# Layer 3 attention of a four-layer network: exponentials turned by block transposes on VectorE and transfers, not by TensorE

## The chip, the cores and the metric

The kernel runs on one core of a Trainium2 chip, which has eight. The metric is the device time of one execution in microseconds (us), as the median of several runs. The profile is of one further execution. The engines of the core are TensorE (PE; its weight loads are shown apart, as PEld), VectorE (DVE), ScalarE (ACT) and GpSimd (POOL). SyncE (SP) computes nothing: it issues transfers (DMAs). Each engine takes its instructions in order from a queue of its own, and they wait for each other by semaphores.

## The reference

The network has four layers on an input of 2 x 512 x 32 x 32 in float32. Layers 0 to 2 are a deformable attention with an MLP, a deformable convolution and a linear attention. The change is in layer 3, an ordinary attention with 8 heads of 64 channels over the 1024 positions of each of the two batch entries:

```python
def _L3_conv_ref(x, gn_scale, gn_bias, W_qkv, b_qkv, W_out, b_out, num_heads):
    ...
    h = _group_norm(x, gn_scale, gn_bias)
    h = jnp.einsum('bchw,cd->bdhw', h, W_qkv) + b_qkv[None, :, None, None]
    h = h.reshape(B, num_heads, 3 * hd, H * W).transpose(0, 1, 3, 2)
    q, k, v = jnp.split(h, 3, axis=-1)
    scale = 1.0 / jnp.sqrt(jnp.asarray(hd, dtype=q.dtype))
    logits = jnp.einsum('bhsd,bhtd->bhst', q, k) * scale
    attn = jax.nn.softmax(logits, axis=-1)
    vals = jnp.einsum('bhst,bhtd->bhsd', attn, v)
    h = vals.transpose(0, 1, 3, 2).reshape(B, C, H, W)
    h = jnp.einsum('bchw,cd->bdhw', h, W_out) + b_out[None, :, None, None]
    return x + h
```

The softmax runs over the keys, so logits are made with queries on the partitions and keys along the row. The product with the values sums over keys, and TensorE sums over partitions. Between the two, each 128 x 1024 block of exponentials has to be turned: keys on the partitions, queries along the row.

## The kernel before, in words

Layers run one after another, with loads and small pieces of the next layer woven in. Layer 3 is the method `heads` of the class `Attention`, called by `layer3`. Its work is a list of 64 items `(b, hp, s0)`: a batch entry, a pair of heads (`hp`, 0 to 3) and 128 queries from `s0`. First come the 32 items of batch entry 0, then those of entry 1. Two items in a row share 256 queries of one pair of heads.

The order of TensorE's instructions is that of the program. That of the other engines is made by a planner of the framework, which goes by what it reckons to be ready, and among what is ready by the order in the program. `issue_after` tells it to queue something behind a given instruction.

One turn of the loop, for item `at`, does this:

- `logits` (L1988) of item `at + 1`: four products of 128 queries with 512 keys, two for each of the two heads, into two tiles `pl` of 128 x 1024 in PSUM. The pool `ps_l` has two such tiles, so the next logits wait until the exponentials of both heads have been read from them.
- `maximum` (L2078) on VectorE: the row maximum of each `pl`, negated.
- `exponentials` (L2086) on ScalarE: exp(pl - max) into a tile `e` in SBUF, with the row sum in `s`.
- `divide` on VectorE: the reciprocal of `s` (L2090) and the row times it (L2091).
- Four groups `g` of four transposes on TensorE (L2040) of item `at`, two groups for each head. Each group goes through a tile `pt` of PSUM and is copied to `aT` in SBUF, by VectorE for one group (L2049) and by ScalarE for three (L2051).
- Behind each group a share of `fill`: other work of TensorE that the stage needs anyway, namely the second batch entry's normalization (L1816 to L1885), values (L1898), queries and keys (L1921), and the output projection (L1951). Its results go through `spare`, one bank of PSUM, and are moved out by VectorE and ScalarE. The projection's results are stored by SP (L1964).
- `weigh` (L2003) once for two items: eight tiles of keys, two heads, with `aT` as the moving operand of 256 queries. The first half runs behind the logits of one turn, the second half behind those of the next. A copy on ScalarE (L2013) takes the result away.

SP has almost nothing to do in this stage: one load of weights and 20 stores.

Of the kernel before, what the change touches and what calls it, by code (L numbers as in the profile page):

```python
# [10 lines left out]
F32 = mybir.dt.float32  # L11
AF = mybir.ActivationFunctionType
ALU = mybir.AluOpType
# [6 lines left out]
HW = 1024  # L20
# [256 lines left out]
def layers(net, out):  # L277
# [12 lines left out]
    with ExitStack() as later:  # L290
# [101 lines left out]
        with ExitStack() as l1:  # L392
# [92 lines left out]
            with ExitStack() as ctx:  # L485
# [5 lines left out]
                for i, _ in enumerate(linear.run(1, bank, held)):  # L491
                    some(keys, 2)
                    some(values, BESIDE[i])
                some(keys, 99)
        layer3(net, att, later, values, banks, out)


# [1339 lines left out]
class Attention:  # L1837
# [129 lines left out]
    def open_heads(self, ctx):  # L1967
        net = self.net
        self.tmp = net.pool(ctx, "l3_tmp", 2)
        self.ps_l = net.psum(ctx, "l3_logits", 2)  # L1970
        self.ps_t = net.psum(ctx, "l3_turn", 2)
        self.ps_o = net.psum(ctx, "l3_out", 1)

    def heads(self, work, first, fill):

        net, nc = self.net, self.net.nc  # L1980
        ident = net.cst("ident")

        def logits(b, hp, s0):
            q, key = self.qk[b, hp, 0], self.qk[b, hp, 1]
            pls = [self.ps_l.tile([128, HW], F32, name="pl", tag="pl") for _ in range(2)]
            for n in range(2):
                for r, pl in zip((0, 64), pls):
                    nc.tensor.matmul(  # L1988
                        pl[:, half(n)],
                        lhsT=q[r : r + 64, s0 : s0 + 128],  # L1990
                        rhs=key[r : r + 64, half(n)],
                        start=True,
                        stop=True,
                    )
            return [(pl, self.maximum(pl)) for pl in pls]

        def weigh(b, hp, s0, aTs):

            po = self.ps_o.tile([128, 256], F32, name="po3", tag="po3")
            for t in range(8):  # L2000
                for r, aT in zip((0, 64), aTs):
                    c0 = 128 * hp + r
                    nc.tensor.matmul(  # L2003
                        po[r : r + 64, :],
                        lhsT=self.v[b][:, t, c0 : c0 + 64],
                        rhs=aT[:, t, :],
                        start=(t == 0),
                        stop=(t == 7),
                        skip_group_check=True,
                    )  # L2010
                if t == 3:
                    yield
            nc.scalar.copy(self.qk[b, hp, 0][:, s0 : s0 + 256], po)  # L2013
            yield

        done = 0
        fill = list(fill)
        weighing = iter(())
        ahead = [self.exponentials(*part) for part in logits(*work[0])]
        for e in ahead:  # L2020
            self.divide(*e)
        for _ in first:
            pass
        for at, (b, hp, s0) in enumerate(work):
            now, ahead = [e for e, _ in ahead], []
            if at + 1 < len(work):
                one, other_one = logits(*work[at + 1])
                ahead.append(self.exponentials(*one))
            next(weighing, None)
            if at % 2 == 0:  # L2030
                aTs = [
                    self.tmp.tile([128, 8, 256], F32, name="aT", tag="aT", bufs=4)
                    for _ in range(2)
                ]
            for g in range(4):
                e, aT = now[g // 2], aTs[g // 2]
                pt = self.ps_t.tile([128, 512], F32, name="pt3", tag="pt3")
                for c in range(4):
                    k = 4 * (g % 2) + c
                    nc.tensor.transpose(  # L2040
                        pt[:, 128 * c : 128 * c + 128], e[:, 128 * k : 128 * k + 128], ident
                    )
                c0 = 128 * (at % 2)
                dst = aT[:, 4 * (g % 2) : 4 * (g % 2) + 4, c0 : c0 + 128]
                src = pt.rearrange("p (c s) -> p c s", s=128)


                if g == 1:
                    evicted = nc.vector.tensor_copy(dst, src)  # L2049
                else:  # L2050
                    evicted = nc.scalar.copy(dst, src)  # L2051
                if ahead and g < 2:
                    with net.tc.issue_after(evicted.ins):
                        if g == 0:
                            ahead.append(self.exponentials(*other_one))
                        else:
                            self.divide(*ahead[1])
                    if g == 0:
                        self.divide(*ahead[0])
                if fill:  # L2060
                    steps, other, count = fill[0]
                    done += 1
                    for _ in range(done * count // (4 * steps) - (done - 1) * count // (4 * steps)):
                        next(other, None)
                    if done == 4 * steps:
                        for _ in other:
                            pass
                        fill.pop(0)
                        done = 0
            if at % 2 == 1:  # L2070
                weighing = weigh(b, hp, s0 - 128, aTs)
        for _ in weighing:
            pass

# [3 lines left out]
        self.net.nc.vector.tensor_reduce(m, pl, AX.X, ALU.max, negate=True)  # L2078
        return m

    def exponentials(self, pl, m):

        nc = self.net.nc
        e = self.tmp.tile([128, HW], F32, name="e3", tag="e3", bufs=4)
        s = self.tmp.tile([128, 1], F32, name="s3", tag="s3", bufs=4)
        nc.scalar.activation(e, pl, AF.Exp, bias=m, accum_out=s)  # L2086
        return e, s

    def divide(self, e, s):
        self.net.nc.vector.reciprocal(s, s)  # L2090
        self.net.nc.vector.tensor_scalar(e, e, s, None, ALU.mult)  # L2091

    def last_bank(self, name):
        return self.ps_t.tile([128, 512], F32, name=name, tag="pt3")
# [2 lines left out]
def layer3(net, att, ctx, values, banks, out):  # L2097


    att.open_heads(ctx)  # L2100
    ps_f = net.psum(ctx, "l3_fill", 1)

    def spare(name):
        return ps_f.tile([128, 512], F32, name=name, tag="fill")

    first = [(0, hp, s0) for hp in range(CC) for s0 in range(0, HW, 128)]
    second = [
        (1, hp, begin + s0)
        for begin, size in ((0, 512), (512, 256), (768, 256))
        for hp in range(CC)  # L2110
        for s0 in range(0, size, 128)
    ]
# [51 lines left out]
```

## Time and profile before

| | us |
|---|---|
| median of 3 runs | 3835.34 (3830.59 to 3837.44) |
| span of the profiled execution | 3835.8 |
| first logits of layer 3 to the end of the span | 3290 to 3836 |
| in these 546 us: PE busy | 528.5 |
| DVE busy | 332.0 |
| ACT busy | 274.3 |
| POOL busy | 0 |

All of the change lies in the last 546 us. The costs of its instructions are read from groups of the same line and shape, and the pace of the stage from the spacing of the logits, which start once for each item. A busy engine in the table is one that has an instruction running; a matmul's end is modelled.

### The profile page before, as it was taken

Reading aid. Unit: us, or ns where it says so; the run is one execution under the profiler, and the core shown is the slowest. Engines: PE = TensorE matmul, PEld = TensorE weight load, DVE = VectorE, ACT = ScalarE, POOL = GpSimd, SP = SyncE. Lnnn points to the kernel's source line nnn. Section 1 sums busy time; section 2 is a strip of 40 time slices with the busy share of each in tenths; the row PEclk is TensorE's granted clock in tenths of the full one; section 3 lists DMA queues with packets and bytes.
Section 4 is the critical chain, followed back from the end, with each engine's and each line's share of the span. In section 5 each row is a group of like instructions: output and inputs, shape, how many; then the busy total and the mean of one; then the engine's idle time right before and its main releaser. Section 6 shows DMA issues by size and latency. Waiting matters only on the chain. (4 is left out here: it accounts for less than half of the span.)

```text
span 3835.8 us, 59384 instructions
## 1 busy us (share of the span) xinstructions
PE 3739.0 (97%) x25356; PEld 1487.3 (39%) x25356; DVE 2765.5 (72%) x3242; ACT 2566.4 (67%) x2941; POOL 189.1 (5%) x180
## 2 busy tenths in 40 slices
PE   7999999999999999999999999999979999899999
PEld 4532222223222322232323444444434544455555
DVE  6999999999999999999999210411475472566565
ACT  7999999999999999999999221211123243345544
POOL 0000000000000000000000000000261150000000
PEclk9999999999999999999999999999999999999999
DMA  3000000000000000000000100112455481000000
GB/s 111 1 23 23 23 1 23 23 23 12 12 23 23 12 12 23 23 12 12 23 23 34 61 0 0 40 61 77 143 185 173 140 276 42 1 12 1 1 20 25
DMA packets 54459, 168.57 MB, mean 44 GB/s; under 512 B 4804, under 2 KB 10436, under 8 KB 51252
## 3 DMA queue, kind: packets, MB, share of 16 engines
q1 hardware_dynamic: 31556, 83.77, 6.2%
q0 software_dynamic: 21776, 79.14, 6.2%
q8 instruction: 200, 3.28, 0.4%
q10 hardware_dynamic: 864, 1.86, 0.2%
q14 instruction: 63, 0.52, 0.0%
HBM read 156.11 MB, written 8.65 MB: 43 GB/s over the span
## 5 line engine op out<-in xcount | busy, mean ns | idle before, releaser
L888 PE MATMUL ph<-h,w_t 128*32 128x512 f32 x16384 | 1808.0, 593 | 15.7 <-ACT lo L898 6.5
L868 DVE TENSOR_TENSOR h<-ab 128x1024 f32<-128x1024 f32 x1024 | 1206.0, 1219 | 67.2 <-PE ph L888 66.2
L888 PEld LDWEIGHTS ph<-h,w_t 128*32 128x32 f32 x16384 | 547.6, 110 | 1239.9 <-issue 1017.2
L877 ACT ACTIVATE h<-h 128x1024 f32<-128x1024 f32 x832 | 872.1, 1067 | 45.6 <-DVE h L868 42.9
L901 DVE SCALAR_TENSOR_TENSOR hi<-lo,low_w,hi 128x1024 f32<-128x1024 f32 x512 | 654.8, 1279 | 31.6 <-ACT hi L900 30.3
L900 ACT ACTIVATE hi<-ph,size_b,size 128x1024 f32<-128x1024 f32 x512 | 621.3, 1214 | 16.7 <-PE ph L888 12.5
L898 ACT ACTIVATE lo<-ph,vec_t 128x1024 f32<-128x1024 f32 x512 | 571.8, 1117 | 5.8 <-PE ph L888 5.4
L2086 ACT ACTIVATE e<-pl,m 128x1024 f32<-128x1024 f32 x128 | 143.6, 1122 | 228.9 <-DVE m L2078 228.9
L1567 PE MATMUL po<-fold,turned 128*128 128x512 f32 x576 | 266.1, 606 | 3.2 <-DVE dfacc L1575 2.9
L2078 DVE TENSOR_REDUCE m<-pl 128x1 f32<-128x1024 f32 x128 | 150.7, 1219 | 147.2 <-PE pl L1988 147.2
L1135 ACT ACTIVATE h<-ph,vec_t 128x512 f32<-128x512 f32 x64 | 44.0, 687 | 312.0 <-PE ph L1127 311.5
L909 PE MATMUL sim<-hi,w 128*32 128x512 f32 x2048 | 251.0, 592 | 0.0
L1127 PE MATMUL ph<-xn,room 128*128 128x512 f32 x512 | 230.9, 594 | 0.0
L1116 PE MATMUL acc<-h,mlp_w_t 128*128 128x512 f32 x512 | 229.8, 592 | 0.0
L1514 DVE SCALAR_TENSOR_TENSOR sum<-got,wts,sum 128x256 f32<-128x256 f32 x432 | 184.4, 478 | 48.8 <-ACT sum L1510 46.4
L1490 POOL DMA_INDIRECT got<-table,idx x144 | 175.0, 1215 | 554.9 <-DVE sum L1514 268.0
L2040 PE MATMUL pt<-cst_t,e 128*128 128x128 f32 x1024 | 149.3, 279 | 6.6 <-ACT aT L2051 4.0
L2040 PEld LDWEIGHTS pt<-cst_t,e 128*128 128x128 f32 x1024 | 118.6, 142 | 93.6 <-issue 61.3
L1567 PEld LDWEIGHTS po<-fold,turned 128*128 128x128 f32 x576 | 106.6, 195 | 112.4 <-issue 107.4
L1116 PEld LDWEIGHTS acc<-h,mlp_w_t 128*128 128x128 f32 x512 | 97.3, 190 | 122.5 <-issue 122.0
L1127 PEld LDWEIGHTS ph<-xn,room 128*128 128x128 f32 x512 | 96.6, 191 | 117.7 <-issue 117.1
L1541 ACT COPY turned<-pt 128x512 f32<-128x512 f32 x72 | 41.9, 582 | 143.8 <-PE pt L1535 143.6
(250 smaller groups left out, 2711.6 us busy)
## 6 DMA issues: line engine op xcount, KB each, us to landing
ab<-feat_d SPq DMA_DIRECT2D x64, 512.0 KB, 4.0
room<-in_dc_w_dram SPq DMA_DIRECT2D x9, 1024.0 KB, 4.8
dc_w_t<-in_dc_w_dram SPq DMA_DIRECT2D x5, 1024.0 KB, 5.3
room<-in_mlp_w_dram SPq DMA_DIRECT2D x1, 4096.0 KB, 15.6
mlp_w_t<-in_mlp_w_dram SPq DMA_DIRECT2D x1, 4096.0 KB, 12.5
dc_w_t<-in_dc_w_dram SPq DMA_DIRECT2D x8, 512.0 KB, 5.0
w_qkv_t<-in_w_qkv_dram SPq DMA_DIRECT2D x3, 1024.0 KB, 8.6
out_dram<-x_all SPq DMA_DIRECT2D x12, 256.0 KB, 2.0
```

Of the source, the lines that this page charges most:

```text
L868: nc.vector.tensor_tensor(h1.rearrange("p (y x) -> p y x", x=32), at_x[:, k : k + 1, :].to_broadcast([128, 32, 32]), at_y[:, k, :].unsquee ...
L877: nc.scalar.activation(h1, h1, AF.Relu)
L888: nc.tensor.matmul(ph[32 * t : 32 * t + 32, half(n)], lhsT=w2[:, c0 : c0 + 32], rhs=pair[t // 2][:, half(n)], start=True, stop=True, skip_ ...
L898: nc.scalar.activation(lo, phs[0], AF.Relu, bias=b2_lo)
L900: nc.scalar.activation(hi, phs[1], AF.Relu, bias=size_b, scale=size)
L901: nc.vector.scalar_tensor_tensor(hi, lo, low_w, hi, ALU.mult, ALU.add)
L909: nc.tensor.matmul(sim[32 * t : 32 * t + 32, half(n)], lhsT=w3[:, 30 - j : 62 - j], rhs=sums[t][:, half(n)], start=(j == 0), stop=(j == 30 ...
L1116: nc.tensor.matmul(accs[oc], lhsT=self.w2[:, m, 128 * oc : 128 * oc + 128], rhs=hs[m], start=(m == 0), stop=(m == 15),)
L1127: nc.tensor.matmul(ph, lhsT=self.w1[:, k, 128 * m : 128 * m + 128], rhs=xn[:, k, :], start=(k == 0), stop=(k == CC - 1),)
L1514: nc.vector.scalar_tensor_tensor(t[:, q, :], g[:, s, :], w, t[:, q, :], ALU.mult, ALU.add)
L1567: nc.tensor.matmul(self.out, lhsT=turned[:, at : at + 128], rhs=self.folded.w[k][:, i, :], start=(k == 0 and i == 0), stop=(k == 8 and i = ...
L2040: nc.tensor.transpose(pt[:, 128 * c : 128 * c + 128], e[:, 128 * k : 128 * k + 128], ident)
```

## The change

TensorE's transposes and their evictions are left out. For each item a new inner function `attend` now makes logits, maxima, exponentials and the division, and then turns both heads' rows:

- ScalarE writes the exponentials in another order, so that the 32-key blocks which will land on the same 32 partitions lie side by side.
- ScalarE divides, in place of VectorE.
- VectorE transposes every 32 x 32 block of the row in place (`nc.vector.transpose`).
- SP moves the blocks to their partitions: 16 transfers for an item, each from 32 partitions to 32 others, two heads of 256 numbers (1 KB) each, 64 KB in all. They go into a tile `aT` that holds two items and two heads.

Both heads' exponentials lie in one tile `e2`, of which there are two buffers; `aT` has two as well. `weigh` reads `aT` with blocks of 32 queries as its inner run. Its first half runs behind the logits of the first of two turns and its second half two groups later in the same turn. The result's pool `ps_o` has two buffers instead of one, and the fill uses the two banks of `ps_t`, which have become free, instead of one of its own.

```diff
-        self.ps_o = net.psum(ctx, "l3_out", 1)
+        self.ps_o = net.psum(ctx, "l3_out", 2)
...
+        turned = {}
...
-            return [(pl, self.maximum(pl)) for pl in pls]
+            return pls
+
+        def attend(at):
+
+            if at % 2 == 0:
+                turned[at // 2] = self.tmp.tile([128, 2, 2, 4, 256], F32, name="aT", tag="aT")
+            e2 = self.tmp.tile([128, 2, HW], F32, name="e3", tag="e3")
+            for r, pl in enumerate(logits(*work[at])):
+                m = self.maximum(pl)
+                e = e2[:, r, :]
+                self.divide(e, self.exponentials(e, pl, m))
+                nc.vector.transpose(e, e)
+            for a in range(4):
+                for u in range(4):
+                    nc.sync.dma_start(
+                        out=turned[at // 2][32 * u : 32 * u + 32, :, at % 2, a, :],
+                        in_=e2[32 * a : 32 * a + 32, :, 256 * u : 256 * u + 256],
+                    )
...
-                        rhs=aT[:, t, :],
+                        rhs=aT[:, r, :, :, 32 * t : 32 * t + 32].rearrange("p s a q -> p (s a) q"),
...
-        ahead = [self.exponentials(*part) for part in logits(*work[0])]
-        for e in ahead:
-            self.divide(*e)
+        attend(0)
         for _ in first:
             pass
         for at, (b, hp, s0) in enumerate(work):
...
             if at + 1 < len(work):
-                one, other_one = logits(*work[at + 1])
-                ahead.append(self.exponentials(*one))
+                attend(at + 1)
             next(weighing, None)
...
             for g in range(4):
-                e, aT = now[g // 2], aTs[g // 2]
-                pt = self.ps_t.tile([128, 512], F32, name="pt3", tag="pt3")
-                for c in range(4):
...
-                if g == 1:
-                    evicted = nc.vector.tensor_copy(dst, src)
-                else:
-                    evicted = nc.scalar.copy(dst, src)
...
+                if g == 2:
+                    next(weighing, None)
                 if fill:
...
-                weighing = weigh(b, hp, s0 - 128, aTs)
+                weighing = weigh(b, hp, s0 - 128, turned.pop(at // 2))
...
+    def exponentials(self, e, pl, m):
+
+        s = self.tmp.tile([128, 1], F32, name="s3", tag="s3", bufs=4)
+        self.net.nc.scalar.activation(
+            e.rearrange("p (u c k) -> p c u k", u=4, k=32),
+            pl.rearrange("p (c u k) -> p c u k", u=4, k=32),
+            AF.Exp,
+            bias=m,
+            accum_out=s,
+        )
+        return s
+
+    def divide(self, e, s):
         nc = self.net.nc
...
+        nc.vector.reciprocal(s, s)
+        nc.scalar.activation(e, e, AF.Copy, scale=s)
...
-    ps_f = net.psum(ctx, "l3_fill", 1)
-
-    def spare(name):
-        return ps_f.tile([128, 512], F32, name=name, tag="fill")
+    spare = att.last_bank
```

More of the change, by code (lines that the diff above doesn't have):

```diff
@@ L1971, in open_heads @@
         self.ps_t = net.psum(ctx, "l3_turn", 2)
-        self.ps_o = net.psum(ctx, "l3_out", 1)
+        self.ps_o = net.psum(ctx, "l3_out", 2)
     def heads(self, work, first, fill):
         net, nc = self.net, self.net.nc
-        ident = net.cst("ident")
+        turned = {}
         def logits(b, hp, s0):
@@ L1994, in logits, with weigh @@
                     )
-            return [(pl, self.maximum(pl)) for pl in pls]
-        def weigh(b, hp, s0, aTs):
-            po = self.ps_o.tile([128, 256], F32, name="po3", tag="po3")
+            return pls
[14 more added lines that the diff above has]
+                    )
+        def weigh(b, hp, s0, aT):
+            po = self.ps_o.tile([128, 512], F32, name="po3", tag="po3")[:, :256]
             for t in range(8):
-                for r, aT in zip((0, 64), aTs):
-                    c0 = 128 * hp + r
+                for r in range(2):
+                    c0 = 128 * hp + 64 * r
                     nc.tensor.matmul(
-                        po[r : r + 64, :],
+                        po[64 * r : 64 * r + 64, :].rearrange("p (a q) -> p a q", q=32),
                         lhsT=self.v[b][:, t, c0 : c0 + 64],
-                        rhs=aT[:, t, :],
+                        rhs=aT[:, r, :, :, 32 * t : 32 * t + 32].rearrange("p s a q -> p (s a) q"),
                         start=(t == 0),
@@ L2024, in heads @@
         for at, (b, hp, s0) in enumerate(work):
-            now, ahead = [e for e, _ in ahead], []
             if at + 1 < len(work):
-                one, other_one = logits(*work[at + 1])
-                ahead.append(self.exponentials(*one))
+                attend(at + 1)
             next(weighing, None)
[L2030 to L2034, printed above, removed]
-            for g in range(4):
-                e, aT = now[g // 2], aTs[g // 2]
-                pt = self.ps_t.tile([128, 512], F32, name="pt3", tag="pt3")
-                for c in range(4):
[L2039 to L2045, printed above, removed]
-                if g == 1:
-                    evicted = nc.vector.tensor_copy(dst, src)
-                else:
[L2051 to L2059, printed above, removed]
+            for g in range(4):
+                if g == 2:
+                    next(weighing, None)
                 if fill:
@@ L2079, in maximum @@
         return m
-    def exponentials(self, pl, m):
-        nc = self.net.nc
[L2084 to L2091, printed above, removed]
+    def exponentials(self, e, pl, m):
[9 more added lines that the diff above has]
+    def divide(self, e, s):
+        nc = self.net.nc
+        nc.vector.reciprocal(s, s)
+        nc.scalar.activation(e, e, AF.Copy, scale=s)
     def last_bank(self, name):
```

## The prediction

> **What bounds the kernel now.** The groups of instructions come first, to find the lines of the layer 3 attention; then their busy time in its stretch; then the order of time.
>
> ```profile
> L2040 PE MATMUL pt<-cst_t,e 128*128 128x128 f32 x1024 | 149.3, 279 | 6.6 <-ACT aT L2051 4.0 <-DVE aT L2049 2.5
> 3340.00:3800.00 460.00, 454.23 (x2566) 244.52 (x2563) 284.35 (x416) 240.06 (x439) 0.00 (x0) 1.00 0.03 10
> 3307.84 1.99 PE L1988 MATMUL pl<-qk 64*128 64x512 f32 x8
> 3809.23 1.99 PE L1988 MATMUL pl<-qk 64*128 64x512 f32 x8
> 3821.58 3.67 PE L2003 MATMUL po<-aT,v 128*64 128x256 f32 x32
> ```
>
> The second line is 460 us from the middle of the stage: TensorE (the first pair) is busy for 454.2, VectorE for 284.4, ScalarE for 240.1, and the granted clock is 1.00. TensorE sets the pace. An item is one call of `logits` (128 queries, two heads); there are 64. Logits of the second item start at 3307.84, of the last at 3809.23: 62 items in 501.4 us, 8.09 each, **16.17 for two** (they share one `weigh`, so two are my unit). From the last logits to the end of the span (3835.8) it is 26.6, and 14.2 of it lie behind the start of the last `weigh`.
>
> **What goes.** The 1024 transposes on TensorE, 149.3 us of 546, or 4.67 for two items; TensorE then has 11.5 of work for two. With them go the evictions of `pt`: 192 on ScalarE at 587 ns, 64 on VectorE at 691. The division (128 at 754 ns) leaves VectorE.
>
> **What comes, per two items.**
> - VectorE: 4 block transposes. No row shows one. Bounds for 128x1024 in f32: 754 ns (the division, L2091, about two elements a cycle) and 2.4 us (two passes). I take 1.2, the row it is nearest to: one element a cycle, L2078 at 1217 in PSUM, L868 at 1219 in SBUF. Sum: 4 maxima at 1.18, 4 reciprocals at 0.16, 4 transposes, and 0.6 of other work: 10.8.
> - ScalarE: 4 divisions, from SBUF to SBUF. Bounds L877, 1060 ns, and L533, 1219; I take 1.10. With exponentials (128x1024, written in another order, taken at the same 1.12 us plus the accumulator's read) and the rest: some 10.2.
> - SP: 32 transfers of 64 KB, one queue. This is the largest sum, so its rows are shown.
>
> ```profile
> 3207.94 0.33 SPq L217 DMA_DIRECT2D wqk_t<-in_wqk_dram  x1
> 3208.31 0.43 SPq L217 DMA_DIRECT2D wv_t<-in_wv_dram  x1
> L520 SPq DMA_DIRECT2D ab<-feat_d x64: 359/420/1047, 67.1 to 1853.8; - x64
> 2919.85 2.15 SPq L1284 DMA_DIRECT2D table<-dwt  x1
> 2922.05 1.85 SPq L1285 DMA_DIRECT2D table<-dwt  x1
> DMA to landing us min/median/max: 1.7/2.0/2.0
> ```
>
> A transfer that follows nothing takes 0.33 us to issue, one right behind another 0.42 to 0.43, and some 0.045 lies between: 0.377 or 0.465 from start to start. I take 0.465, since in a burst of sixteen fifteen follow another. So SP needs 32 x 0.465 = **14.9** for two items, more than any engine. The two `table` lines are far dearer, and they alone move 32 partitions, as the change's do. They stand behind 1.75 MB that was issued 1 us earlier, and I read them as queued behind its data. The last line is for L1964 (128 to 256 KB to memory): I take 2.0 from issue to landing, bounds 1.7 and 4.0 (L520's median, 512 KB). Data don't bind: the four `table` transfers, 2 MB, land 9.5 us after the first issue, 4.7 per MB, while an item moves 1 MB in 7.4 of issue.
>
> The Trainium skill ("SBUF — State Buffer", Door 1: The DMA port swizzle) speaks against blocks of 32 partitions: they reach 8 of 16 ports, 189 GB/s at 1 MiB instead of 328. An estimate by it is 5.5 us for an item's 1 MiB, which is still under the issue, so the sum would be unchanged.
>
> **The path that sets the end.** `e2` has two buffers. The exponentials of item n+2 overwrite what the sixteen transfers of item n read, so one round of a buffer is: exponentials, divisions, transposes, transfers, landing. What is queued behind that wait on ScalarE is everything behind those exponentials: their second half, divisions and the evictions of the fill. TensorE waits for it through `ps_l`. The handoffs come from here:
>
> ```profile
> 3294.33 2.36 DVE L2078 TENSOR_REDUCE m<-pl 128x1 f32<-128x1024 f32 x2 [1.72 <-PE pl L1988]
> 3296.60 0.68 DVE L1907 TENSOR_TENSOR v<-pv,b_v_row_t 128x512 f32<-128x512 f32 x1
> 3297.20 0.15 DVE L2090 RECIPROCAL s<-s 128x1 f32<-128x1 f32 x1
> 3295.59 1.11 ACT L2086 ACTIVATE e<-pl,m 128x1024 f32<-128x1024 f32 x1 [22.65 <-DVE m L2078]
> 3296.72 1.11 ACT L2086 ACTIVATE e<-pl,m 128x1024 f32<-128x1024 f32 x1
> 3297.73 0.19 ACT L2086 ACTIVATION_READ_ACCUMULATOR e<-pl,m 128x1 f32 x1
> ```
>
> The second exponential starts 1.15 behind the first and is read out 1.20 later; 0.05 to the first division; that ends after 1.10, the first transpose starts 0.15 later and the second follows it: 1.10 + 0.15 + 2 x 1.2 = 3.65, and the second division hides under it; 0.10 to SP; fifteen issues, 6.98; landing of the last, 2.0; 0.15 back to ScalarE. **Sum 15.28 for two items** (each buffer holds every second one). The lines show one thing more: `v` (L1907), written behind the reciprocal in the program, runs ahead of it, so the planner orders VectorE by what it thinks is ready. I therefore take both maxima ahead of the first reciprocal, as here, and not the order in which `attend` writes them, which would serialize two heads.
>
> Three additions.
> - The two items of a pair collide on SP. `weigh` now runs wholly in the first of each two iterations, and needs all transfers of the pair. From their landing TensorE does half of it (1.88), fill (0.95; two items' 3.8 in four parts), the other half and fill, 5.66, then the other item's logits, whose first exponential starts 3.27 later (2.02 to the maximum, 1.25 to the exponential). So its round starts 8.93 behind, not 7.64, its burst ends 8.93 + 6.15 + 7.44 = 22.52 after the start of the first, and the next burst, due at 15.28 + 6.15 = 21.43, waits 1.09 in one round and less in the next: 0.55 on the mean.
> - Evictions of the fill (some 2 for two items at 0.69) fall between the steps: 0.3.
> - TensorE's clock. It now idles while it waits for landings:
>
> ```profile
> 3312.85 1.28 PE L2040 MATMUL pt<-cst_t,e 128*128 128x128 f32 x8 [2.00 <-ACT aT L2051]
> 3314.06 3.44 PE L1988 MATMUL pl<-qk 64*128 64x512 f32 x8
> 3313.70:3317.00 3.30, 3.30 (x11) 1.22 (x9) 0.92 (x2) 1.17 (x4) 0.00 (x0) 0.50 0.02 5
> ```
>
> After 2.00 us of idling the granted clock was 0.50 for 3.3 us, and logits took 3.44, not 1.99. By the round above, the stall ahead of `weigh` is about 2.6: logits of the next item can start at 8.93 + 2.35 = 11.3, end at 13.2, and the landing is at 15.8. Should half the stretches behind it run at half clock (1.7 us of loss, half of it taken up by the other buffer's slack), it is 0.4 to 0.5; I take 0.5, with bounds 0 and 1.7.
>
> The Trainium skill ("TensorE: Matmul & The Clock Gate", Why this matters for your kernels) warns only of idle gaps above some 3 us. By its rule this stall is free and the estimate would be 16.1 for two items, 3840 in all; the trace's gap of 2.00 says otherwise.
>
> **Sum.** 15.28 + 0.55 + 0.3 + 0.5 = 16.6 for two items against 16.17: 31 x 0.43 = +13. The end: 3.27 + 15.1 from the last logits to the landing, then the 14.2 that stay: 32.6 against 26.6, +6. TensorE's 4.67 are won, and a chain through SP takes their place. Span 3835.8 + 19 = **3855**; the profiled execution lies 0.5 above the median of the runs, so the same holds for that.
>
> **Rivals.**
> 1. Issue at the lone price. 0.377 makes SP 12.1 and the round 13.96; with 0.85 for collisions and evictions and no loss of clock, 14.8. Then 31 x -1.37 = -42, +5 at the end: 3798. For it: these transfers have half the rows of L217's, and L1964 costs 332 ns every time. Against: every second one in a row in this trace costs 0.42 or more. From 0.43 down the kernel is faster. A transpose of 754 ns would not add much: TensorE's order alone asks 11.3 + 3.27 = 14.55.
> 2. Order on VectorE: the planner puts the next item's two maxima ahead of an item's last transposes. It orders by its own estimates, and VectorE's queue is in order; each such case delays the burst by 2.36, the round becomes 18.96, +86 +6: 3928. For it: L1907 above; against: the transposes stand earlier in the program, and seem to be ready about when the maxima are. It decides from a delay of some 0.5 us up. Transposes of two passes (2.4) come to the same.
> 3. The 32-partition form itself costs what L1284 and L1285 show (1.3 to 2.15): 32 x 1.7 = 54 for two items, some 5000 in all. Against: a backlog explains them.
>
> **How the numbers follow.** Two runs of this kernel are told apart by about 0.2%, 7.7 us. Chances: the forecast 0.46 (0.36 slower, 0.10 within), rival 1 0.34 (0.32 faster, 0.02 within), rival 2 0.15, rival 3 0.05: faster 0.32, same 0.12, slower 0.56. The forecast's own range is 3830 to 3885 (clock loss and landing at their bounds). The range over the cases goes from rival 1 at its best (14.55 for two items, 3788) to rival 2: 3785 to 3935, with rival 3 and little else outside.
>
> **What would show it.** Right: SP's issues back to back for most of the stage at 0.42 each, first exponentials that wait for transfers, TensorE at some 70% with waits on transfers at L2003's line, 0.50 stretches of the clock, two items at 16.6. Wrong: issues at 0.33, or TensorE busy throughout (then rival 1); maxima between an item's two transposes (rival 2); issues above 1 us (rival 3). A transpose off 1.2, or a landing off 2.0, breaks the round at that term.

## The result, and the profile after

| | before | after |
|---|---|---|
| median of 4 runs each, side by side | 3832.97 | 4024.39 (4022.45 to 4026.3) |
| ratio after to before | | 1.05, 95% interval 1.0485 to 1.0514 |
| span of the profiled execution | 3835.8 | 4020.6 |
| second logits to last logits (62 items) | 501.4 | 669.1 |
| for two items | 16.17 | 21.58 |
| last logits to the end | 26.6 | 48.9 |

The change costs 191 us; the forecast was +19, and the range ended at 3935. The sign was right and the size was not. The 184.8 us between the two spans divide as follows. The 62 items take 167.7 more and the end 22.3 more, and the stage starts 5.2 earlier (second logits at 3302.6, not 3307.8). Of the 167.7, one gap of 40.12 between two logits holds 23.8, for an ordinary gap at that place is 16.4. The other 144 are 31 x 4.64.

First the groups of instructions of the kernel after (busy time, mean ns | idle time just before and what ended it), then the list of its transfers (size, us to landing):

```profile
L2015 PE MATMUL po<-aT,v 128*64 128x256 f32 x1024 | 177.8, 508 | 159.7 <-DMA aT<-e 159.7
L2065 ACT ACTIVATE e<-pl,m 128x1024 f32<-128x1024 f32 x128 | 141.9, 1111 | 279.9 <-DMA aT<-e 189.8
L2002 DVE STREAM_TRANSPOSE e<-e 128x1024 f32<-128x1024 f32 x128 | 151.8, 1224 | 55.4 <-ACT e L2077 42.3
...
aT<-e SPq DMA_DIRECT2D x1024, 64.0 KB, 2.0
```

TensorE's 149 us of transposes are gone, but the weighing (L2015) now stands idle for 159.7 us, all of it until a transfer has landed, and the exponentials (L2065) wait 189.8 us for transfers to have read their buffer. The transpose itself is 1224 ns, and a transfer lands 2.0 us after its issue. So these two steps are as cheap as they were reckoned; what lies between them is a queue. Next the middle of the stage by busy time (PE, PEld, DVE, ACT, POOL, then granted clock, DMA share and GB/s), and what the view of the transfers' own line says:

```profile
3340.00:3730.00 390.00, 293.95 (x1088) 120.63 (x1085) 191.83 (x232) 179.35 (x257) 0.00 (x0) 0.85 0.42 101
...
L2005 SPq DMA_DIRECT2D aT<-e x1024: 585/595/1542, 3296.2 to 4000.9; - x171
DMA to landing us min/median/max: 2.0/2.0/3.8
```

No computing engine is the bound: TensorE is at 75%, VectorE at 49%, ScalarE at 46%, the DMA engines at 42%. The line below is the answer. One issue on SP lasts 595 ns at the median and never less than 585; from start to start it is 0.639. Thirty-two of them are 20.45 us, where two items in the undisturbed middle (the 5th to the 43rd logits) take 21.04. Counted from start to start, SP, which computes nothing, is taken up for 97% of the time. The chain of waits, read backwards from the last instruction, shows the same as a share of the whole span, by engine and then by tile and line:

```profile
SPq 12%; PE 11%; DVE 3%; DMA 3%; issue 1%; ACT 1%; POOL 0%; DVEq 0%; ACTq 0%; POOLq 0%
SPq L2005 12%; PE po L1567 3%; PE pq L1921 1%; DMA got<-table,idx 1%; PE pw L1445 1%; PE po L2015 1%; DVE sum L1514 1%; PE pv L1898 1%; PE pf L1951 1%; DMA aT<-e 1%; DVE m L2059 0%; DVE e L2002 0%; PE pt L1535 0%; PE pl L1984 0%; PE pqk L1662 0%
```

In order of time one sees how the queue holds both ends. The timeline of the kernel after (start, us, engine, line; in brackets the idle time before and what ended it):

```profile
3554.93 30.56 SPq L2005 DMA_DIRECT2D aT<-e  x47
...
3568.23 2.37 DVE L2002 STREAM_TRANSPOSE e<-e 128x1024 f32<-128x1024 f32 x2 [0.87 <-DMA aT<-e]
3570.53 2.32 DVE L2059 TENSOR_REDUCE m<-pl 128x1 f32<-128x1024 f32 x2
3574.92 1.11 ACT L2065 ACTIVATE e<-pl,m 128x1024 f32<-128x1024 f32 x1 [5.68 <-DMA aT<-e]
3575.01 3.49 PE L2015 MATMUL po<-aT,v 128*64 128x256 f32 x16 [5.81 <-DMA aT<-e]
```

In this window 47 issues fill 30.56 us, 0.65 each. At 3574.9 the same landing releases the exponentials of one item and the weighing of another, each after more than 5 us of idling. The half of a weighing behind that gap takes 3.49 us, where 1.95 is usual at full clock: from 3574.9 to 3578.2 the granted clock was 0.50 (the 0.85 above is the mean of the middle).

The gap of 40.12 and the end have the same cause:

```profile
3746.33 2.37 DVE L2002 STREAM_TRANSPOSE e<-e 128x1024 f32<-128x1024 f32 x2 [0.87 <-DMA aT<-e]
3762.08 0.57 SPq L1869 DMA_DIRECT2D w_out_t<-in_w_out_dram  x1
3767.18 2.07 PE L1951 MATMUL pf<-qk,w_out_t 128*128 128x512 f32 x2 [21.17 <-DMA w_out_t<-in_w_out_dram]
...
3980.13 21.37 SPq L2005 DMA_DIRECT2D aT<-e  x32
4003.41 6.04 PE L2015 MATMUL po<-aT,v 128*64 128x256 f32 x32 [13.88 <-DMA aT<-e]
```

The load of the output projection's weights (L1869) is one instruction of SP. It stands behind all transfers that were issued before it, goes out at 3762.08, and TensorE, which has the first projection next in its order, stands still for 21.17 us. At the end SP is two items behind: from 3980.13 on it issues the 32 transfers of the last two, TensorE idles 13.88 us for them, and the last weighing starts 31.7 us after the last logits (3971.74).

### The profile page after: what moved, and what is told of

It is laid out like the page before. It is cut to its first block, busy times and chain, and to the rows that moved or that the text cites. A ratio compares the mean times of both kernels' runs of the same rounds, so it can differ in the third digit from the quotient of the medians.

```text
span 4020.6 us, 58924 instructions
## 1 busy us (share of the span) xinstructions
PE 3730.5 (93%) x24332; PEld 1421.8 (35%) x24332; DVE 2778.8 (69%) x3178; ACT 2597.7 (65%) x2877; POOL 189.6 (5%) x180
## 5 line engine op out<-in xcount | busy, mean ns | idle before, releaser
L2015 PE MATMUL po<-aT,v 128*64 128x256 f32 x1024 | 177.8, 508 | 159.7 <-DMA aT<-e 159.7
L2065 ACT ACTIVATE e<-pl,m 128x1024 f32<-128x1024 f32 x128 | 141.9, 1111 | 279.9 <-DMA aT<-e 189.8
L1984 PE MATMUL pl<-qk 64*128 64x512 f32 x512 | 168.9, 654 | 28.0 <-ACT e L2065 26.6
L2002 DVE STREAM_TRANSPOSE e<-e 128x1024 f32<-128x1024 f32 x128 | 151.8, 1224 | 55.4 <-ACT e L2077 42.3
L2015 PEld LDWEIGHTS po<-aT,v 128*64 128x64 f32 x1024 | 95.9, 180 | 259.4 <-issue 230.3
## 6 DMA issues: line engine op xcount, KB each, us to landing
mlp_w_t<-in_mlp_w_dram SPq DMA_DIRECT2D x1, 4096.0 KB, 12.3
```

Of the source, the lines that this page charges most:

```text
L2015: nc.tensor.matmul(po[64 * r : 64 * r + 64, :].rearrange("p (a q) -> p a q", q=32), lhsT=self.v[b][:, t, c0 : c0 + 64], rhs=aT[:, r, :, :, ...
```

## The experiments

The theory after this reading is that SP pays a fixed price of some 0.6 us for each transfer from SBUF to SBUF, and that its 32 issues for two items are the bound. Rivals are that the price belongs to 32 partitions or to the bytes, that the chain of an item (exponential, division, transpose, transfer, landing) is the bound and SP is only full, and that the division on ScalarE is what costs.

**What a transfer costs by itself.** This kernel computes no layer; it only issues bursts of twelve transfers of each form from SP, ScalarE and GpSimd.

```diff
+        for queue, tag in ((nc.sync, "sp"), (nc.scalar, "act"), (nc.gpsimd, "pool")):
+            form(f"{tag}_s32x2x256", queue, 12, lambda t, i: (as4(t)[row_of(i, 1), 0:2, at2(i)], v[quarter(i), 0:2, at2(i)]))
...
+            form(f"{tag}_s32x4x256", queue, 12, lambda t, i: (as4(t)[row_of(i, 1), 0:4, at2(i)], v[quarter(i), 0:4, at2(i)]))
+            form(f"{tag}_s128x128", queue, 12, lambda t, i: (t[:, 128 * i : 128 * i + 128], src[:, 128 * i + 128 : 128 * i + 256]))
...
+            form(f"{tag}_h32x2x256", queue, 12, lambda t, i: (as4(t)[row_of(i, 1), 0:2, at2(i)], hv[quarter(i), 0:2, at2(i)]))
+            form(f"{tag}_h128x128", queue, 12, lambda t, i: (t[:, 128 * i : 128 * i + 128], hbm[:, 128 * i + 128 : 128 * i + 256]))
```

> Computes none of the layers: it loads the input, stores it as the output, and issues bursts of twelve transfers of each of seven forms on each of three queues (SP, ACT, POOL): 32 partitions x 2 x 256 numbers from SBUF to SBUF (the change's form), 32 x 512, 32 x 4 x 256 (128 KB), 128 x 128, 128 x 2 x 64, and 32 x 2 x 256 and 128 x 128 from HBM to SBUF. If the price is that of the change's form (32 partitions, or SBUF at both ends), then on SP that form costs about 0.595 us each as in the changed kernel, and the 128-partition forms or those from HBM 0.33 to 0.43. If it is a price of any transfer in a dense burst, all forms cost about 0.6. On POOL, which is idle in the stage, I expect 0.5 to 1.2 each.

Its source view lists each form with count and minimum, median and maximum in ns (names are cut: `s32x2x` is 32 partitions from SBUF, two rows of 256 each, as in the change; `h` is from main memory):

```profile
L2155 SPq DMA_DIRECT2D sp_s32x2x<-src x12: 585/596/740, 8.0 to 26.1; - x12
L2155 SPq DMA_DIRECT2D sp_s32x4x<-src x12: 600/607/633, 34.4 to 41.5; - x12
L2155 SPq DMA_DIRECT2D sp_s128x<-src x12: 599/600/609, 42.2 to 49.3; - x12
L2155 SPq DMA_DIRECT2D sp_h32x2x<-hbm x12: 413/425/526, 58.0 to 63.3; - x12
L2155 SPq DMA_DIRECT2D sp_h128x<-hbm x12: 320/436/587, 63.7 to 69.7; - x12
L2155 ACTq DMA_DIRECT2D act_s32x2x<-src x12: 592/607/737, 62.7 to 72.3; - x12
L2155 POOL DMA_DIRECT2D pool_s32x2x<-src x12: 539/539/559, 98.6 to 104.5; - x12
```

On SP and ScalarE the price goes with the kind of transfer. From SBUF to SBUF it is 588 to 620 ns on SP in all five shapes, for 32 partitions or 128 and for 64 KB or 128 KB; from main memory to SBUF it is 425 and 436 in two of these shapes. ScalarE's queue is no cheaper than SP's, and GpSimd's is by a tenth; there the source makes no difference, for the change's shape from main memory costs 541 on the mean. From start to start the change's form takes 0.639 on SP and the same form from main memory 0.470.

Nor is it a price of following another transfer, as the 0.42 was in the rows that the prediction read. In the version with larger transfers, below, the first issue of each of 31 bursts comes after more than 7 us without one and still takes 585 to 595 ns. SBUF as the source alone isn't it either: a store from SBUF to main memory that follows nothing takes 332 ns (L1964 before the change).

**Price per transfer or per byte.** Each transfer is cut in two, with the same bytes and rows.

```diff
-                    nc.sync.dma_start(
-                        out=turned[at // 2][32 * u : 32 * u + 32, :, at % 2, a, :],
-                        in_=e2[32 * a : 32 * a + 32, :, 256 * u : 256 * u + 256],
-                    )
+                    for r in range(2):
+                        nc.sync.dma_start(
+                            out=turned[at // 2][32 * u : 32 * u + 32, r, at % 2, a, :],
+                            in_=e2[32 * a : 32 * a + 32, r, 256 * u : 256 * u + 256],
+                        )
```

> The changed kernel with each 64 KB transfer of the turning cut in two of 32 KB: 64 transfers for two items, the same bytes in the same 1 KB rows. Theory A (SP pays for each transfer, some 0.62 to 0.64 us from start to start whatever its size): 64 x 0.63 = 40.3 per two items against 20.45, so 31 x 19.9 = +615 us: about 4640 (4560 to 4700). Theory B (SP is held up by the data: 64 KB take 0.64 us): the same bytes, the same time, 4024 +- 30, with issues of some 0.3.

Measured: 4662.31 in one run, and two items take 40.97. The transfers' line of this kernel:

```profile
L2006 SPq DMA_DIRECT2D aT<-e x2048: 507/588/1619, 3303.2 to 4641.8; - x187
```

Half the bytes, and 588 ns instead of 595. The price is for the transfer.

**Does the chain of an item matter?** The block transposes are left out, so that the blocks are moved unturned and each item's chain is 2.4 us shorter.

```diff
-                nc.vector.transpose(e, e)
```

> Leaves out the block transposes on VectorE (the attention's weights of layer 3 then stand in untransposed blocks); all transfers stay. Theory A (SP's issue is the bound): no change, within 10 of 4024, since 2.4 us of the round are removed where SP is busy anyway. Rival C (the latency of a round through two buffers is the bound, as I had predicted it): 2.37 less for each round of two items, 31 x 2.37 = 73 less: 3951.

Measured: 4023.69, ratio 1.0495 (1.0472 to 1.0517) against 1.05 for the change itself. Leaving out 152 us of VectorE's work and 2.4 us of every round brings nothing. The chain only waits for SP.

**Half of the transfers on another queue.**

```diff
-                    nc.sync.dma_start(
+                    (nc.sync, nc.gpsimd)[a // 2].dma_start(
                         out=turned[at // 2][32 * u : 32 * u + 32, :, at % 2, a, :],
```

> Half of an item's transfers go to POOL's queue, which is idle in this stage; nothing else differs. Theory A (SP's issue sets the pace, 32 x 0.639 = 20.5 us for two items): SP then needs 10.2 for two items, the round of a buffer falls by 8 x 0.639 = 5.1 to some 13 to 14, and TensorE's order asks 14.5 to 16.5 for two: 31 x -5 = -155, with the load of w_out waiting for less and an end some 8 shorter: 3850, 3820 to 3900, if POOL issues in at most 0.64; at 1.2 each POOL is the bound at 19.2 and the gain is some 40. Theory B (the data of 32-partition transfers, on half of the ports, set the pace): no change, 4024.

Measured: 3811.04 (3809.42 to 3812.69), ratio 0.994 (0.992 to 0.9961). The same bytes, transposes and divisions, issued from two queues, and 213 us are gone; the kernel is now 0.6% faster than before the change. Two items take 15.05. It is 9 us below the range that was expected. In the middle of the stage TensorE is busy 362.54 of 390 us, at a granted clock of 0.99:

```profile
3340.00:3730.00 390.00, 362.54 (x1505) 148.49 (x1504) 268.04 (x327) 244.41 (x352) 216.06 (x412) 0.99 0.53 149
```

The Trainium skill ("Perfetto Trace Analysis", What "DMA-bound" means) names an issuing queue that is solid with issues as a bound apart from the DMA engines. By the same page (DMA Optimizations), spreading the issues over several engines may help in that case. This case agrees: the engines' share was 0.42 beside a full SP, and the split took 213 us.

**The load behind the transfers.** Only the load of `w_out` leaves SP.

```diff
-        self.net.nc.sync.dma_start(out=self.w_out, in_=self.net.ins["w_out"])
+        self.net.nc.gpsimd.dma_start(out=self.w_out, in_=self.net.ins["w_out"])
```

> The load of w_out alone is moved from SP's queue to POOL's, which is idle. Theory: TensorE's 21 us of idling at the first output projection come from the place of this load behind two items' transfers on SP. Then the gap goes, 15 to 24 us less: 4000 to 4009. If SP's total issue time alone sets the end, the gap was only borrowed from the later waits for transfers and the time stays within 5 of 4024.

Measured: 4009.07, ratio 1.0455 (1.0433 to 1.0477), 15.3 below the change. The gap of 40.12 between two logits is 16.4 here, an ordinary one, and the largest anywhere is 19.13. So 15 of the 191 us are one instruction's place in a queue. The gap was 24 us longer than its neighbours; in the two profiled executions the 62 items differ by 17.9 (669.1 and 651.2), so some 6 of the 24 come back in the items behind it, probably because SP works through its backlog during the gap.

**The division.** Two kernels: the change with the division back on VectorE, and the kernel before with the division alone moved to ScalarE. The edit of the first is shown; the second is its reverse, in the kernel before.

```diff
-        nc.scalar.activation(e, e, AF.Copy, scale=s)
+        nc.vector.tensor_scalar(e, e, s, None, ALU.mult)
```

> The changed kernel with the division alone put back on VectorE. Theory (SP's 32 issues set the pace of the stage, 20.45 of 21 per two items, so no part of an item's own chain matters): no change, 4024 (4015 to 4033). Rival (the division holds up the second exponential on ScalarE here too, as it did when it alone was moved in the kernel before, at 0.65 us per item): 64 x -0.65 = -40, about 3984.

> The kernel before with the division alone moved from VectorE to ScalarE, its TensorE transposes kept. Theory (TensorE sets the pace there, and neither of the two engines reaches two thirds of the stage): ScalarE rises by 4 x 1.09 = 4.4 of 16.17 per two items, VectorE falls by 3.0, and the time stays: 3833, 3825 to 3845. Rival (the division's longer way on ScalarE, 1.09 against 0.75, and its place in ScalarE's queue behind the next exponential delay the transposes): +0.3 to +0.6 per item, 3855 to 3870.

In the change: 4030.88, ratio 1.0514 (1.0497 to 1.0532); putting the division back saves nothing. In the kernel before: 3874.12, ratio 1.0106 (1.0087 to 1.0124), 40 us for this part alone. Here the rival was right in kind and I was not (40 us, where it allowed up to 37), though TensorE sets the pace and ScalarE stays under three quarters of the time. ScalarE's order in time, first of the kernel with the division moved:

```profile
3504.43 1.12 ACT L2086 ACTIVATE e<-pl,m 128x1024 f32<-128x1024 f32 x1 [2.38 <-DVE m L2078]
...
3505.86 1.15 ACT L2091 ACTIVATE e<-e,s 128x1024 f32<-128x1024 f32 x1 [0.23 <-DVE s L2090]
...
3507.65 1.13 ACT L2086 ACTIVATE e<-pl,m 128x1024 f32<-128x1024 f32 x1
```

and of the kernel before:

```profile
3504.54 1.11 ACT L2086 ACTIVATE e<-pl,m 128x1024 f32<-128x1024 f32 x1 [3.45 <-DVE m L2078]
...
3506.28 1.12 ACT L2086 ACTIVATE e<-pl,m 128x1024 f32<-128x1024 f32 x1
```

With the division in ScalarE's queue the second exponential starts 3.22 us after the first, not 1.74, since the division, the copy of a weighing's result and an eviction come between. The later exponential is not what TensorE waits for: none of its logits (L1988) stands idle for one. It waits for ScalarE's evictions of `pt`, which now queue behind the divisions. The group of the transposes shows it, in the kernel with the division moved (before, its idle time was 6.6, of it 4.0 for L2051):

```profile
L2040 PE MATMUL pt<-cst_t,e 128*128 128x128 f32 x1024 | 154.8, 282 | 31.6 <-ACT aT L2051 28.1 <-DVE aT L2049 2.9
```

That is 25 us more of idling and 5.5 more of busy time, 30.5 of the 32.8 by which the two profiled spans differ (3868.6 and 3835.8); two items take 17.37. So an engine that is busy for 71% of the time (327.79 of 460 us) can still hold up the one that sets the pace, by the order of its queue. In the kernel after the change the two exponentials go first and the divisions behind them, as its timeline shows, so this cost is not in its time:

```profile
3574.92 1.11 ACT L2065 ACTIVATE e<-pl,m 128x1024 f32<-128x1024 f32 x1 [5.68 <-DMA aT<-e]
...
3576.03 1.10 ACT L2065 ACTIVATE e<-pl,m 128x1024 f32<-128x1024 f32 x1
...
3577.12 2.18 ACT L2077 ACTIVATE e<-e,s 128x1024 f32<-128x1024 f32 x2
```

**Fewer, larger transfers.** Both items of a pair share a buffer, and 16 transfers of 128 KB replace 32 of 64 KB; `aT` then has room for one buffer only.

```diff
-                turned[at // 2] = self.tmp.tile([128, 2, 2, 4, 256], F32, name="aT", tag="aT")
-            e2 = self.tmp.tile([128, 2, HW], F32, name="e3", tag="e3")
+                turned[at // 2] = self.tmp.tile([128, 2, 2, 4, 256], F32, name="aT", tag="aT", bufs=1)
+                both[at // 2] = self.tmp.tile([128, 2, 2, HW], F32, name="e3", tag="e3")
+            e2 = both[at // 2]
...
+            if at % 2 == 0:
+                return
             for a in range(4):
                 for u in range(4):
                     nc.sync.dma_start(
-                        out=turned[at // 2][32 * u : 32 * u + 32, :, at % 2, a, :],
-                        in_=e2[32 * a : 32 * a + 32, :, 256 * u : 256 * u + 256],
+                        out=turned[at // 2][32 * u : 32 * u + 32, :, :, a, :].rearrange(
+                            "p r s q -> p (r s) q"
+                        ),
+                        in_=e2[32 * a : 32 * a + 32, :, :, 256 * u : 256 * u + 256].rearrange(
+                            "p r s q -> p (r s) q"
+                        ),
```

> The changed kernel with both items of a pair in one buffer of exponentials, so that one transfer carries both items (128 KB, four rows of 256 elements from each of 32 partitions) and 16 replace 32 for two items; the turned buffer is single for want of space. Theory A (a price per transfer): issue falls to 16 x 0.65 = 10.4 per two items; what binds next is the round of the two pair buffers and the single turned buffer, some 16.5 to 17 per two items: 3860 (3830 to 3900). Theory B (SP is held up by the bytes): SP stays at 20 per two items and the single turned buffer makes it worse: 4024 or more.

Measured: 3955.68, ratio 1.0314 (1.0297 to 1.0331): better than the change, but not the 3860 expected. The timeline of this kernel, from one weighing to the next:

```profile
3505.52 3.36 PE L2022 MATMUL po<-aT,v 128*64 128x256 f32 x16 [3.70 <-DMA aT<-e]
3509.86 1.95 PE L2022 MATMUL po<-aT,v 128*64 128x256 f32 x16
...
3511.85 10.30 SPq L2008 DMA_DIRECT2D aT<-e  x16
...
3524.12 1.95 PE L2022 MATMUL po<-aT,v 128*64 128x256 f32 x16 [2.10 <-DMA aT<-e]
```

Sixteen transfers of twice the size issue in 10.30 us, 0.644 each: the price per transfer once more. But with one `aT` the burst can't start until the weighing has read it (3511.8), and the weighing can't start until the burst has landed: 6.3 + 10.3 + 2.0 = 18.6, one after the other (the 2.0 from the end of the last issue). The 16.5 to 17 that I expected for two items is too low for that round; two items take 19.48. One bound was exchanged for another.

**With SP out of the way: what is next?** The split version was taken further: each half of a weighing is placed one item apart, so that the wait for the last landing falls behind other work, and `w_out` and the result's stores go to GpSimd's queue as well. In the diff `attend` ends with the transposes, and `turn` holds the 16 transfers, 8 on SP and 8 on GpSimd's queue. Then the same without the block transposes, and the same with the blocks sent by way of main memory.

```diff
...
+            e2 = attend(at + 1) if at + 1 < len(work) else None
+            next(weighing, None)
             if at + 1 < len(work):
-                attend(at + 1)
-            next(weighing, None)
+                turn(at + 1, e2)
             for g in range(4):
-                if g == 2:
-                    next(weighing, None)
...
```

> The changed kernel with each item's transfers split over two queues (8 on SP, 8 on GpSimd's), with w_out and the stores of the result on GpSimd's queue, and with the second half of each weighing one item later, so that the wait for the last landing falls behind other work. Theory (what is left after the split, 14.7 per two items, is TensorE waiting at the weighing for landings): the round of a buffer, 15.28 with 16 issues of one queue, becomes 1.15 + 1.20 + 0.05 + 3.65 + 0.10 + 7 x 0.64 + 2.0 + 0.15 = 12.8, so 13.0 to 13.6 per two items: 31 x -1.3 = -40 from 3811, about 3772 (3755 to 3795). Rival (landings are not what is waited for; the order of exponentials and evictions on ScalarE sets the 14.7): 3805 to 3815.

> The version with two queues and a later weighing, without the block transposes on VectorE (left out; the blocks are moved unturned). Theory (with SP relieved the chain of an item decides again: maxima stand behind the transposes of the item before on VectorE, a cycle of 6.9 an item, and the round of a buffer holds two transposes as well): it falls to TensorE's own 11.5 to 12.3 per two items, 3803 - 31 x 1.7 = 3750 (3735 to 3770). Rival (transfers and landings still decide, whatever stands ahead of them): 3795 to 3810, as leaving them out of the changed kernel made no difference.

Measured: 3803.0, ratio 0.9921 (0.9902 to 0.9939), 14.64 for two items; and without the transposes 3751.74, ratio 0.979 (0.9774 to 0.9806), 13.05 for two items. The first is the fastest complete version here, though the interval doesn't part it from the plain split, and it missed its 3772 and came out just below the rival's 3805 to 3815. The second has the time that was expected (3750), but not the 11.5 to 12.3 for two items that the expectation named. VectorE in order of time, in the version with the transposes:

```profile
3508.66 2.37 DVE L2000 STREAM_TRANSPOSE e<-e 128x1024 f32<-128x1024 f32 x2 [0.87 <-ACT e L2081]
3510.96 2.32 DVE L2063 TENSOR_REDUCE m<-pl 128x1 f32<-128x1024 f32 x2
...
3515.58 2.37 DVE L2000 STREAM_TRANSPOSE e<-e 128x1024 f32<-128x1024 f32 x2 [0.87 <-DMA aT<-e]
3517.88 2.32 DVE L2063 TENSOR_REDUCE m<-pl 128x1 f32<-128x1024 f32 x2
```

The maxima of an item queue behind the transposes of the one before: 6.92 from one to the next, 13.84 for two items. In the trace 44 of the 63 steps from one item's maxima to the next take no more than 7.2 us, so this order is the bound most of the time. In 7 of the 19 longer ones the exponentials wait 2.9 to 4.7 us for transfers; what makes the other twelve longer stays open. The run without transposes agrees: the instruction that brought nothing when it was left out of the change brings 51 us here. That run doesn't tell this order from the round of a buffer of exponentials, which holds the transposes too.

By way of main memory (`there` is a tile in it), one store and eight loads of an item take the place of 16 transfers:

```diff
...
+            there = self.there.tile([128, 2, HW], F32, name="there", tag="there")
+            nc.sync.dma_start(out=there, in_=e2)
             for u in range(4):
+                for r in range(2):
+                    nc.sync.dma_start(
+                        out=turned[at // 2][32 * u : 32 * u + 32, r, at % 2, :, :],
+                        in_=there[:, r, 256 * u : 256 * u + 256].rearrange("(a k) q -> k a q", k=32),
+                    )
...
```

> The version with a later weighing, its blocks turned by way of the chip's main memory: per item one store of 1 MB and eight loads of 128 KB back, all on SP, in place of 16 transfers of 64 KB on two queues. Theory (the price of some 0.6 us belongs to transfers from SBUF to SBUF; from main memory it is 0.43, start to start 0.47, and for a store 0.33): SP needs 2 x (0.4 + 8 x 0.47) = 8.3 per two items on one queue, the buffer of exponentials is free when the store has landed, and VectorE's chain of maxima and transposes (6.9 an item in the version with two queues) sets the pace: 3790 (3765 to 3825). Rival (twice the bytes: the two-queue version moves 153 GB/s at a share of 0.55, 278 GB/s at a share of 1, and 4.2 MB per two items need 15.1 us at that): 3835 to 3880.

Measured: 3919.9, ratio 1.0223 (1.0206 to 1.024), worse than the rival's 3835 to 3880. Issues last what they should, but landings are far longer. Its windows row and the landing of its loads:

```profile
3340.00:3700.00 360.00, 271.92 (x1132) 123.51 (x1134) 199.43 (x243) 186.96 (x271) 0.53 (x1) 0.88 0.85 230
...
L2011 SPq DMA_DIRECT2D aT<-there x512: 302/430/2614, 3302.5 to 3898.9; - x171
DMA to landing us min/median/max: 2.6/4.7/8.6
```

The issue is 430 ns, and 338 for the store, which reads SBUF too. The DMA engines are at 0.85, and a landing is 4.7 us, not 2.0; it comes twice in an item's chain, for a load must follow the store's landing. Whether the engines' 0.85 or this longer chain sets the 18.43 for two items, no run here separates.

## Why the prediction was wrong in size

**The step that failed** is the term of SP's issue: 32 x 0.465 = 14.9 for two items. Measured it is 32 x 0.639 = 20.45. Moving half of the issues to another queue took 213 us, which shows that this term decides. The forecast was a chain through a buffer's round, 15.28, with SP just under it. With the measured price the round would be 15.28 + 15 x 0.174 = 17.9, and SP's 20.45 is above that: the bound is not the round but the queue. The forecast named the right place and the wrong kind of limit, and so its additions (0.55 for collisions, 0.3, 0.5) went where nothing was decided.

The 0.465 was not misread. It is what transfers from main memory cost on SP, 0.470 in the bursts. No row of the trace of before moves data from SBUF to SBUF, and I took the rows of another kind as if the kind didn't matter. Nor does the difference between a lone transfer and one behind another, on which the forecast and the first rival were parted, exist for this kind (585 to 595 ns for the first of a burst). My prices on either side, 0.377 and 1.3 to 2.15, enclose 0.639, but I had explained the upper one away and made it a rival at 0.05. With 0.639 the forecast's own arithmetic gives 31 x (20.45 - 16.17) = +133 and +6 at the end, 3975. From there to 4020.6 it is 24 for the gap at the first projection, 16 more at the end, 11 for the 0.36 by which two items are above 20.45 (20.81, the 669.1 less 23.8 over 31), less 5 at the start. A range over the bounds of the price would have held the time. A term at 92% of the old pace (14.9 of 16.17), with a price taken from another kind of transfer, should have set the upper end of the range.

**A part that was left out**: what else stands in SP's queue. The load of `w_out` costs 15.3 (shown by moving it alone). The end is 48.9 where I had 32.6. Of these 16.3, 13.3 lie ahead of the last weighing, which starts 31.7 after the last logits and not 18.4: I had counted one item's burst, and it was SP's backlog of two. The other 3.0 lie behind its start, and 2.4 of them are the weighing itself (6.04 us, not 3.67).

**What held.** Transposes: 1.224, taken at 1.2. Division on ScalarE: two in 2.18, taken at 1.10 each. Landing: 2.0. Exponentials: 1.11 apart in the timeline, taken at 1.15. First exponentials that wait for transfers, and TensorE at 75% with waits at the weighing, were named as signs (some 70%). Issues came back to back, as named, but at 0.595 and not at 0.42, and two items were not at 16.6. The clock: 0.85 in the middle of the stage, which I had costed at 0.5 for two items; while SP is the bound it probably costs little, since TensorE waits for transfers anyway; no run shows that alone.

**The rivals.** The first, cheaper issue, is wrong in its cause, and that its 3798 is near where the kernel goes once SP no longer binds (3811 and 3803) is a coincidence. The second, maxima between two transposes, did not come: the transposes of all 64 items run in pairs (2.37 for two). The third, a price for 32 partitions, is wrong: 128 partitions cost the same 600 ns. What makes these transfers a kind of their own is that both ends lie in SBUF: a load from main memory took SP 0.43 to 0.44 in the bursts and a store that follows nothing 0.33, where this kind takes 0.585 or more in either place. What made the two `table` rows of 1.3 to 2.15 dear, no run here shows.

## What to carry to other kernels

Count a new stream of transfers first as instructions of the queue that issues them, at the price of their own kind (here SBUF to SBUF), and if no row of that kind exists, carry both bounds into the range as soon as the sum comes near the pace of the stage. A queue that is nearly full also delays whatever else stands in it: list its loads and stores, and put them, or half of the stream, on another queue. And the worth of an instruction on one engine is that of the bound of the moment: the same block transposes were worth nothing in one version and 51 us in the next.

## What the runs showed of the hardware

- An issue of a transfer from SBUF to SBUF costs SP 0.596 us (0.639 from start to start), ScalarE 0.607 and GpSimd 0.539; from main memory to SBUF SP needs 0.425 (0.470), ScalarE 0.441 and GpSimd 0.54; a store from SBUF to main memory that follows nothing takes SP 0.33. Partitions and size hardly count: 588 ns for 32 KB, 596 for 64 KB, 607 for 128 KB, 600 for 128 partitions.
- A transfer of this kind landed after 1.8 us for 32 KB, 2.0 for 64 KB and 2.3 for 128 KB, so halving or doubling its size moved landing little. With two queues issuing side by side it rose to 2.5 and 2.6 for SP's.
- A transpose of 32 x 32 blocks in float32 on VectorE takes 1.224 us for 128 x 1024, in place, as long as a maximum of the same size (1.208), where the division takes 0.754.
